# Masks and the first maximum behind self-attention's last turning, and the keys of batches 2 to 5 one step sooner

## The chip, the cores and the metric

The kernel runs on one core of a Trainium2 chip. The metric is the time of one execution in microseconds (us), taken on the device. Besides the plain timed runs there is one profiled execution, whose trace gives every instruction of every engine with its start and duration: TensorE (PE), VectorE (DVE), ScalarE (ACT), GpSimd (POOL), and SyncE (SP), which only issues DMAs.

## The reference

A stack of four attention blocks over x (8 batches, 256 positions, width 128) with a context of 8 x 64 x 64. The first two and the last are single cross-attention blocks. Nearly all of the work is the third, a decoder of six layers, each of which does:

```
tn = _ln(t, norm_g, norm_b)
t  = _mha(tn, tn, skv, sq, sow, sob, tgt_mask) + t      # self-attention, 16 heads of 64, 256 x 256 scores
tn = _ln(t, norm_g, norm_b)
t  = _mha(src, tn, ckv, cq, cow, cob, src_mask) + t     # cross-attention, 256 queries on 64 context rows
tn = _ln(t, pg, pb)
t  = t + (relu(tn @ w1 + b1) @ w2 + b2)                 # feed-forward, 512 wide
```

In `_mha` the scores are `q k^T / 8`, set to -1e9 where the mask is 0, then softmax, times the values, times the output weights. All is float32.

## The kernel before

**How work is put in order.** Every step of the kernel is a small Python function, put into a plan with `at(tick, phase, fn)`. At the end the plan is played by tick, and within a tick by phase, and the instructions of each engine are chained in just that order. So the order on each engine is written out by hand; what a step waits for beyond that follows from the data and from the buffers. Every PSUM tile, one or two banks, comes from one pool of four tiles (`psum`, line 30), which `two_banks`, `mm_tile` and `tp_tile` take in turn: a new tile waits until the one four places before it has been read out. SBUF tiles of 1024 columns come from a heap with four tiles for each tag ("q", "k", "v", "e", "o").

**A layer** has 48 ticks: self-attention takes four ticks for each of the eight batches, cross-attention two, from the tick that is called `T_ca`; its last stages, and the feed-forward, lap over into what follows.

**Self-attention** (`plan_sa`), for batch b at tick T. Two groups g of heads, four parts jj each. `scores` (PE, L946) fills a PSUM tile; `exps` adds the mask and takes the minimum (DVE, L960) and exponentiates (ACT, L965); `divide` takes the reciprocal (DVE, L973) and scales (POOL, L975, four instructions a part); `turn` transposes 32 x 32 blocks on DVE into `eTc` (L985, two instructions a part, each of which needs two of POOL's four scalings); `values(g)` (PE, L1001, 64 matmuls of two passes) multiplies with V into two PSUM tiles in turn, four matmuls to the first, four to the second, and so on; DVE copies the first out (L309) and ACT the second (L311). Then the output weights (L1019) and the sum with the residual (DVE, L1026). For the last batch, the last turn stands at tick `T_ca`, phase 2.2, and `values(1)` at tick `T_ca + 1`, phase 3.0.

**Cross-attention** (`plan_ca`, `plan_weights_64`), for batch b at T = T_ca + 2b:
- `keys_both` (for two batches, b even): folded keys on PE (L1138) into two PSUM tiles of two banks, copied by ACT (L1144, four instructions) into two "q" tiles.
- `mask_keys`: a tensor_tensor (L1152) that adds the context mask to the last 32 partitions of the batch's 1024 key columns, in place, on DVE.
- For each half qt of the queries at tick T + qt: `scores` (PE, L366, phase 1) into a PSUM tile; `lower` at phase 2, which copies it to SBUF (ACT, L377), takes the maximum of each head (DVE, L379) and subtracts it (POOL, L380); `exps` (ACT, L386, phase 8); one tick later `divide`, the sum and reciprocal (DVE, L390, L391) and the scaling (POOL, L392); two ticks later `turn` (DVE, L400); three ticks later `sums` (PE, L434) and the sum into t (DVE, L1170).
- `make_values` (PE, L328; ACT, L334), and `ahead`, the layer norm: statistics on DVE (L856 to L862), scale on POOL (L866, L869), normal form on ACT (L875), turned on PE (L889, tile `tp`) and copied by ACT (L891).

The mask of batch 0 stands at tick T_ca - 1, phase 1.9, and that of batch 1 at T_ca, phase 1.9. The keys of 2 and 3 stand at T_ca + 2, phase 3.7, their masks at T_ca + 3 and T_ca + 4, phase 1.9; the keys of 4 and 5 at T_ca + 6, phase 3.7.

Of the kernel before, what the change touches and what calls it, by code (L numbers as in the profile page):

```python
# [27 lines left out]
def tile_xattn_stack(ctx: ExitStack, tc: tile.TileContext, io, out: bass.AP):  # L28
    nc = tc.nc
# [15 lines left out]
    def two_banks(base):  # L45
        return psum.tile([P, 1024], F32, tag="ps", name=uniq(base))
# [10 lines left out]
    def big(tag, bufs=4, shape=(P, 1024), dtype=F32):  # L57

        return heap.tile(list(shape), dtype, tag=tag, name=uniq(tag), bufs=bufs)
# [244 lines left out]
    def at(tick, phase, fn):  # L304
        plan.setdefault(tick, []).append((phase, fn))
# [7 lines left out]
    def residual(b, bias):  # L313
        tb = sb([P, QT, D], "tb", 3)
        nc.gpsimd.tensor_tensor(
            tb, tt(b), bias.unsqueeze(1).to_broadcast([P, QT, D]), ALU.add
        )
        return tb

    def values_of(b, wvo):  # L320

        ps = two_banks("mm").rearrange("p (r k x) -> p r k x", r=2, k=2)
        w = wvo.rearrange("p (g a) d -> p a g d", g=2)
        for k in range(2):
            for a in range(4):
                for r in range(2):
                    rows = slice(r * DM, (r + 1) * DM)
                    nc.tensor.matmul(  # L328
                        ps[32 * a : 32 * a + 32, r, k, :],
                        lhsT=ctx2[rows, b, 32 * k : 32 * k + 32],  # L330
                        rhs=w[rows, a], start=True, stop=True,
                    )
        vw = big("v", shape=(P, 2, 2, 2, D))
        nc.scalar.copy(  # L334
            vw.rearrange("p r k g d -> p (r k g d)"), ps.rearrange("p r k x -> p (r k x)")
        )
        return vw

    def plan_weights_64(tick, qt, qT, keys, values, halves, take):

# [95 lines left out]
            take(ps)  # L438

        at(tick, 1, scores)  # L440
        at(tick, 2, lower)
        if halves:
            at(tick + 1, 2.05, exps)
            at(tick + 1, 2.5, turn)
# [245 lines left out]
    def plan_l0(b, T):  # L690
# [88 lines left out]
        for qt in range(QT):  # L779
            plan_weights_64(  # L780
                T + qt, qt, lambda: st["q"], lambda: st["k"], lambda: st["VW"], True,
                lambda ps, qt=qt: add(qt, ps),
            )
# [342 lines left out]
    def plan_ca(l, b, T):  # L1126
        st = {}
        fold = W["fold", l]

        def keys_both():  # L1130

            res = [big("q", shape=(D, 4, 4, M)) for _ in range(2)]
            for g in range(2):
                ps = two_banks("mm").rearrange("p (r a x) -> p r a x", r=2, a=4)
                for a in range(4):
                    for r in range(2):
                        rows = slice(r * DM, (r + 1) * DM)
                        nc.tensor.matmul(  # L1138
                            ps[:, r, a, :], lhsT=fold["AT"][rows, 4 * g + a, :],
                            rhs=ctx2[rows, b : b + 2, :].rearrange("p b m -> p (b m)"),  # L1140
                            start=True, stop=True,
                        )
                for i in range(2):
                    nc.scalar.copy(  # L1144
                        res[i][:, :, 2 * g : 2 * g + 2, :].rearrange("p a r k -> p r a k"),
                        ps[:, :, :, i * M : (i + 1) * M],
                    )
            keys_of[b], keys_of[b + 1] = res

        def mask_keys():  # L1150
            last = keys_of[b][96:].rearrange("p a c k -> p (a c) k")
            nc.vector.tensor_tensor(  # L1152
                last, last, nm2[96:, b].unsqueeze(1).to_broadcast([32, 16, M]), ALU.add
            )

        def make_values():
            st["VW"] = values_of(b, fold["WVO"])

        def res():
            st["tb"] = residual(b, W["ca", l][3])  # L1160

        ahead(b, (T - 5, 6), (T - 3, 2.95), (T - 2, 2.9), last_off, last_on, st)
        if b % 2 == 0:
            at(T - 2, 3.7, keys_both)
        at(T - 1 - b % 2, 1.9, mask_keys)
        at(T + 2, 3.2, make_values)
        at(T + 2, 7, res)

        def add(qt, ps):
            nc.vector.tensor_add(t[:, QT * b + qt, :], ps[:, :D], st["tb"][:, qt, :])  # L1170

        for qt in range(QT):
            plan_weights_64(
                T + qt, qt, lambda: st["tT"], lambda: keys_of[b], lambda: st["VW"],
                False, lambda ps, qt=qt: add(qt, ps),
            )

    def plan_ff(l, b, T, T_second, steps=None):
# [117 lines left out]
    for l in range(NL):  # L1296
        T_ca = T0 + 4 * B
        T_next = T_ca + 2 * B
        for b in range(B):
            plan_sa(l, b, T0 + 4 * b)  # L1300
        plan_ca_weights(l, T_ca - 7)
        for b in range(B):
            plan_ca(l, b, T_ca + 2 * b)
            T_ff = T_ca + 2 * b + 7
            if l + 1 < NL:
                plan_ff(l, b, T_ff, T_ff + 2)
            elif b < B - 2:
                plan_ff(l, b, T_ff, T_ff + 1)
            else:

                T_ff -= b - B + 3
                done = T_ca + 2 * b + 4
                plan_ff(
                    l, b, T_ff, T_ff + 1,
                    (4.6, (done, 6), (done, 8.7), (T_ff, 2.9)),
                )
            T_end[b] = T_ff + 1
        if l > 0:
            at(T0 + 8, -1, lambda l=l: load_ff(l))
        if l + 1 < NL:  # L1320
            at(T_ca + 4, -1, lambda l=l: load_sa(l + 1))
            at(T_next + 1, -1, lambda l=l: load_ca(l + 1))
        T0 = T_next
# [82 lines left out]
```

## Time and profile before

| what | value |
|---|---|
| plain runs | 2408.59, 2408.69 and 2411.47 us, median 2408.69 |
| the profiled execution | 2410.73 us |
| its span, first to last instruction | 2409.0 us |
| busy: PE, DVE, ACT, POOL | 2300.7, 1922.7, 1720.0, 1398.4 us |
| mean granted TensorE clock | 0.985 |
| one layer | 368.56 us |

The profiled execution is what every duration is taken from. "Busy" is the time in which an engine ran at least one instruction; PE's matmuls are pipelined, so a busy PE need not be at its peak, and a float32 matmul is recorded as two passes. The granted clock is the share of full speed that the chip let TensorE have; at 0.5 its matmuls take twice as long. In the timeline a row has its start, its length, the engine, the source line, the operation, the tiles (out<-in), the shapes and the count, and in brackets how long the engine stood idle before it and whose result ended that. In a view of windows a row has, for one stretch, its length, the busy time of PE, PE's weight loads, DVE, ACT and POOL with their instructions, the granted clock, and the DMA's share and rate.

### The profile page before, as it was taken

How to read it: one execution, taken by the hardware profiler on the slowest of the kernel's cores; microseconds unless marked ns; L12 is line 12 of the kernel's file. 1: busy time of each engine (PE TensorE's matmuls, PEld its weight loads, DVE VectorE, ACT ScalarE, POOL GpSimd, SP SyncE). 2: the span in 40 equal slices, each digit the busy share in tenths (PEclk: the TensorE clock that was granted, in tenths of full speed). 3: DMA queues.
4: the chain of work that ended last, by engine and by line, in shares of the span. 5: the costliest groups of instructions: out<-in, count | busy, mean ns of one | idle time of the engine just before them, and what ended most of it. 6: DMA issues, size and time to landing. Idle time of an engine off the chain costs nothing.

```text
span 2409.0 us, 97481 instructions
## 1 busy us (share of the span) xinstructions
PE 2300.7 (96%) x41124; PEld 1696.1 (70%) x41124; DVE 1922.7 (80%) x6269; ACT 1720.0 (71%) x4544; POOL 1398.4 (58%) x2243
## 2 busy tenths in 40 slices
PE   7889999999998999998999999899999899999897
PEld 3557776777776777776677777677777677777675
DVE  5678888967888967888877888877888877888885
ACT  4567777767777677777677778677778668777663
POOL 2445556854555864555865555865555774555774
PEclk9989999999999999999999999999999999999998
DMA  6000012001012001012001012000012000010000
GB/s 180 2 12 15 21 56 65 2 3 30 21 50 60 12 3 30 21 43 68 12 3 30 21 38 71 14 2 18 25 38 73 21 2 18 25 38 12 2 4 16
DMA packets 98932, 70.67 MB, mean 29 GB/s; under 512 B 7936, under 2 KB 93632, under 8 KB 98496
## 3 DMA queue, kind: packets, MB, share of 16 engines
q1 hardware_dynamic: 97904, 64.12, 9.9%
q8 instruction: 323, 5.29, 1.0%
q14 instruction: 113, 0.93, 0.1%
q10 hardware_dynamic: 592, 0.33, 0.1%
HBM read 59.19 MB, written 5.24 MB: 27 GB/s over the span
## 4 chain that ended last, share of the span: by engine, by line
PE 80%; DVE 11%; ACT 6%; issue 1%; POOL 1%; DMA 1%; SPq 0%; ACTq 0%; POOLq 0%; DVEq 0%
PE mm L909 14%; PE sc L946 13%; PE mm L1001 13%; PE mm L1019 7%; PE mm L928 7%; PE mm L434 6%; PE sc L366 4%; PE mm L1203 4%; PE mm L1186 3%; DVE m L379 2%; PE mm L328 2%; DVE e L960 2%; PE tp L889 2%; ACT e L965 1%; PE mm L1138 1%
## 5 line engine op out<-in xcount | busy, mean ns | idle before, releaser
L975 POOL TENSOR_SCALAR e<-e,rs 128x256 f32<-128x256 f32 x1536 | 714.8, 485 | 724.7 <-DVE rs L973 714.8
L965 ACT ACTIVATE e<-e,mn 128x256 f32<-128x256 f32 x1536 | 758.5, 495 | 145.5 <-DVE mn L960 144.6
L960 DVE CUSTOM_DVE_ANT_0 e<-sc,nm 128x256 f32<-128x256 f32 x1536 | 543.4, 419 | 116.7 <-PE sc L946 115.3
L985 DVE STREAM_TRANSPOSE eTc<-e 128x512 f32<-128x512 f32 x768 | 513.8, 693 | 54.0 <-POOL e L975 53.1
L1001 PE MATMUL mm<-eTc,v 32*64 32x256 f32 x12288 | 372.7, 385 | 25.1 <-DVE eTc L985 25.1
L946 PE MATMUL sc<-k,q 64*32 64x256 f32 x12288 | 380.5, 382 | 1.4 <-ACT v L311 0.6
L1001 PEld LDWEIGHTS mm<-eTc,v 32*64 32x64 f32 x12288 | 283.8, 134 | 111.0 <-issue 44.3
L380 POOL TENSOR_TENSOR e<-e,m 128x1024 f32<-128x1024 f32 x112 | 213.1, 1902 | 207.1 <-DVE m L379 206.8
L946 PEld LDWEIGHTS sc<-k,q 64*32 64x32 f32 x12288 | 221.7, 107 | 122.9 <-issue 45.9
L965 ACT ACTIVATION_READ_ACCUMULATOR e<-e,mn 128x1 f32 x1536 | 287.7, 187 | 0.0
L379 DVE TENSOR_REDUCE m<-e 128x16 f32<-128x1024 f32 x112 | 136.4, 1218 | 102.4 <-ACT e L377 100.3
L434 PE MATMUL mm<-v,o 128*128 128x128 f32 x1536 | 192.8, 279 | 18.7 <-DVE o L400 11.5
L434 PEld LDWEIGHTS mm<-v,o 128*128 128x128 f32 x1536 | 178.9, 192 | 41.4 <-issue 26.9
L909 PE MATMUL mm<-tT,w_sk 128*128 128x256 f32 x768 | 189.3, 389 | 0.0
L1019 PEld LDWEIGHTS mm<-w_sow,o 128*128 128x128 f32 x1536 | 175.1, 192 | 19.0 <-issue 12.3
L311 ACT COPY v<-mm 128x1024 f32<-128x1024 f32 x96 | 97.2, 1012 | 124.8 <-PE mm L928 124.8
L1019 PE MATMUL mm<-w_sow,o 128*128 128x128 f32 x1536 | 183.6, 278 | 2.8 <-ACT WVO L1100 2.8
L366 PE MATMUL sc<-q,tT 128*32 128x256 f32 x3072 | 185.5, 382 | 0.3 <-DVE t L1170 0.3
L928 PE MATMUL mm<-w_sv,tT 128*32 128x256 f32 x3072 | 185.6, 382 | 0.0
L392 POOL TENSOR_TENSOR e<-e,r 128x1024 f32<-128x1024 f32 x96 | 182.6, 1902 | 0.5 <-DVE r L391 0.5
L909 PE MATMUL mm<-tT,w_sq 128*128 128x256 f32 x768 | 173.6, 379 | 0.0
L909 PEld LDWEIGHTS mm<-tT,w_sk 128*128 128x128 f32 x768 | 138.2, 190 | 44.2 <-issue 29.2
(226 smaller groups left out, 3457.6 us busy)
## 6 DMA issues: line engine op xcount, KB each, us to landing
nm<-mask_d SPq DMA_DIRECT2D x192, 128.0 KB
w_sk<-in_L_sa_kv_dram SPq DMA_DIRECT2D x6, 512.0 KB
w_sv<-in_L_sa_kv_dram SPq DMA_DIRECT2D x24, 128.0 KB
w_sq<-in_L_sa_q_dram SPq DMA_DIRECT2D x6, 512.0 KB
w_sow<-in_L_sa_ow_dram SPq DMA_DIRECT2D x6, 512.0 KB
w_ckv<-in_L_ca_kv_dram SPq DMA_DIRECT2D x12, 256.0 KB
w_cq<-in_L_ca_q_dram SPq DMA_DIRECT2D x6, 512.0 KB
w_cow<-in_L_ca_ow_dram SPq DMA_DIRECT2D x6, 512.0 KB
```

Source lines behind the costliest of these rows:

```text
L366: nc.tensor.matmul(sc[32 * a : 32 * a + 32, q, :], lhsT=qT()[:, qb * 32 : (qb + 1) * 32], rhs=keys()[:, a].rearrange("p h k -> p (h k)"), ...
L380: nc.gpsimd.tensor_tensor(e, e, m.unsqueeze(2).to_broadcast([P, 16, M]), ALU.subtract)
L434: nc.tensor.matmul(ps[:, :D], lhsT=eT[:, s].rearrange("p q x -> p (q x)"), rhs=vw[:, r, k, g, :], start=(s == 0), stop=(s == 7),)
L909: nc.tensor.matmul(ps[:, i * S : (i + 1) * S], lhsT=w[:, c * P : (c + 1) * P], rhs=st["tT"], start=True, stop=True,)
L928: nc.tensor.matmul(ps[32 * a : 32 * a + 32, i, :], lhsT=st["tT"][:, kb * 32 : (kb + 1) * 32], rhs=sv[:, a].rearrange("p g x -> p (g x)"), ...
L946: nc.tensor.matmul(sc[32 * a : 32 * a + 32, r, j, :], lhsT=st["q"][g][rows, a, qb * 32 : (qb + 1) * 32], rhs=st["k"][g][rows, a, :], start ...
L960: nc.vector.tensor_tensor_reduce(e[:, i, :], sc4[:, i, :], st["nm"][:, 2 * jj + i % 2, :], -1.0, 3.0 * BIG, ALU.add, ALU.min, mn[:, i : i ...
L965: nc.scalar.activation(e[:, i, :], e[:, i, :], AF.Exp, scale=-1.0, bias=mn[:, i : i + 1], accum_out=rs[:, i : i + 1],)
L975: nc.gpsimd.tensor_scalar(e[:, i, :], e[:, i, :], rs[:, i : i + 1], 1.0, ALU.mult, ALU.mult)
L985: nc.vector.transpose(eT[:, r, :, 2 * jj : 2 * jj + 2, :], e[:, 2 * r : 2 * r + 2, :].rearrange("p j (k x) -> p k j x", x=32),)
L1001: nc.tensor.matmul(ops[a // 2][r * HD : (r + 1) * HD, a % 2, :S], lhsT=st["v"][kb // 4][rows, kb % 4, (2 * g + r) * HD : (2 * g + r + 1) * ...
L1019: nc.tensor.matmul(st["ps"][:, j * D : (j + 1) * D], lhsT=st["oT"][c // 4][:, c % 4, j * P : (j + 1) * P], rhs=sow[:, c, :], start=(c == 0 ...
```

## The change

```diff
-    def plan_weights_64(tick, qt, qT, keys, values, halves, take):
+    def plan_weights_64(tick, qt, qT, keys, values, halves, take, lower_at=2):
...
         at(tick, 1, scores)
-        at(tick, 2, lower)
+        at(tick, lower_at, lower)
...
         def mask_keys():
             last = keys_of[b][96:].rearrange("p a c k -> p (a c) k")
-            nc.vector.tensor_tensor(
+            (nc.vector if b else nc.gpsimd).tensor_tensor(
                 last, last, nm2[96:, b].unsqueeze(1).to_broadcast([32, 16, M]), ALU.add
             )
...
         if b % 2 == 0:
-            at(T - 2, 3.7, keys_both)
-        at(T - 1 - b % 2, 1.9, mask_keys)
+            at(*{2: (T - 3, 2.95), 4: (T - 3, 3.7)}.get(b, (T - 2, 3.7)), keys_both)
+
+        at(
+            *{0: (T - 1, 2.2), 1: (T - 2, 5.5), 2: (T - 2, 1.9), 3: (T - 4, 5.5)}.get(
+                b, (T - 1 - b % 2, 1.9)
+            ),
+            mask_keys,
+        )
...
             plan_weights_64(
                 T + qt, qt, lambda: st["tT"], lambda: keys_of[b], lambda: st["VW"],
                 False, lambda ps, qt=qt: add(qt, ps),
+                2.25 if b == 0 and qt == 0 else 2,
             )
```

In each of the six layers:
- The mask of batch 0 goes from DVE to POOL, at the same tick (T_ca - 1), phase 2.2.
- The mask of batch 1 stays on DVE and in tick T_ca, but at phase 5.5 instead of 1.9.
- `lower` of batch 0's first half goes from phase 2 to 2.25 of tick T_ca, so its copy, maximum and subtraction are issued after the last turn (phase 2.2) of self-attention.
- The keys of batches 2 and 3 go from T_ca + 2, phase 3.7, to T_ca + 1, phase 2.95, just ahead of self-attention's last `values(1)`; their masks go to T_ca + 2, phases 1.9 and 5.5.
- The keys of batches 4 and 5 go from T_ca + 6 to T_ca + 5, phase 3.7; their masks and those of 6 and 7 stay.

No instruction is added or removed but for the engine of the one mask. On DVE the new order around the last turn is: turn (L985, both), maximum (L379), mask of batch 1 (L1152), next maximum. On PE it is: scores, `tp`, scores, keys (L1138, two tiles), `values(1)`. On ACT the four key copies now come after the second L377 and before the copy (L311) that follows `values(1)`.

## The prediction

> **What bounds the kernel now.** I read the page first, then who waits for whom on the TensorE, then the timeline of the worst wait, then clock windows around it.
>
> ```profile
> PE 2300.7 (96%) x41124; PEld 1696.1 (70%) x41124; DVE 1922.7 (80%) x6269; ACT 1720.0 (71%) x4544; POOL 1398.4 (58%) x2243
> ...
> PE 80%; DVE 11%; ACT 6%; issue 1%; POOL 1%; DMA 1%; SPq 0%; ACTq 0%; POOLq 0%; DVEq 0%
> ```
>
> PE is the bound: only gaps in its queue, or its clock, can be won. Its waits (total us, times, longest):
>
> ```profile
> PE mm L1001 <- DVE eTc L985: 25.1, 12, 3.1
> ...
> PE mm L434 <- DVE o L400: 11.5, 12, 1.6
> PE mm L434 <- DVE t L1170: 6.3, 6, 1.1
> ```
>
> Times below are of layer 0; the layers repeat every 368.56 us (the 3.11 us wait ends at 404.98, 773.54 and so on to 2247.78). Where self-attention passes into cross-attention the timeline has
>
> ```profile
> 399.94 1.93 PE L366 MATMUL sc<-q,tT 128*32 128x256 f32 x32
> ...
> 400.33 1.27 DVE L985 STREAM_TRANSPOSE eTc<-e 128x512 f32<-128x512 f32 x2
> 400.51 2.80 POOL L975 TENSOR_SCALAR e<-e,rs 128x256 f32<-128x256 f32 x4 [0.19 <-DVE rs L973]
> ...
> 401.63 1.33 DVE L1152 TENSOR_TENSOR q<-q,nm 32x1024 f32<-32x1024 f32 x1
> 403.00 1.22 DVE L379 TENSOR_REDUCE m<-e 128x16 f32<-128x1024 f32 x1
> ...
> 404.13 1.29 DVE L985 STREAM_TRANSPOSE eTc<-e 128x512 f32<-128x512 f32 x2
> 404.29 1.90 POOL L380 TENSOR_TENSOR e<-e,m 128x1024 f32<-128x1024 f32 x1
> ...
> 404.98 5.89 PE L1001 MATMUL mm<-eTc,v 32*64 32x256 f32 x128 [3.11 <-DVE eTc L985]
> ...
> 406.23 1.06 ACT L386 ACTIVATE e<-e 128x1024 f32<-128x1024 f32 x1 [4.80 <-POOL e L380]
> 407.19 0.99 ACT L377 COPY e<-sc 128x1024 f32<-128x1024 f32 x1
> ```
>
> A mask (L1152) and the first maximum (L379) stand ahead of the last turning (404.13), and PE stands from 401.87 to 404.98. The values then take 5.89 us; the same 64 matmuls took 3.71 at 394.06. The windows (PE busy first, granted clock after POOL) say why:
>
> ```profile
> 402.60:406.00 3.40, 1.02 (x23) 0.64 (x31) 2.79 (x4) 0.00 (x0) 3.28 (x4) 1.00 0.00 0
> 406.00:409.40 3.40, 3.40 (x77) 2.56 (x69) 1.18 (x2) 2.73 (x4) 0.20 (x1) 0.50 0.02 5
> 409.40:412.80 3.40, 3.40 (x87) 1.98 (x72) 3.21 (x9) 1.54 (x2) 3.28 (x2) 1.00 0.00 0
> ```
>
> After a window that is 30% busy the clock is halved for the next 3.41 us: 1.7 us lost. The other 0.4 is the second half of the turning.
>
> **First mask to POOL.** DVE loses 1.22 us at 393.00. Its next work, L960, needs the first half of L946 (392.18 to 394.13), so it starts at 393.2 instead of 394.25. POOL's scaling before it ends at 393.60 instead of 394.56, since one of its instructions took 1.44 instead of 0.48 beside that mask. The mask takes 1.90 on POOL by L380 (the same 1024 columns, two SBUF operands), from 0.73 (L315) to 3.80 (twice L380). It waits for ACT's third key copy, which ends at 392.96, before POOL is free, and behind it stand only scalings. POOL has nothing to do until 397.4 and PE wants the keys at 397.70, so all of these are hidden; past 4.1 us each one costs one.
>
> **The last turning.** DVE's copy L309 now waits for PE's values (397.75, was 398.29). The statistics behind it take 1.96 as now, so the second reciprocal comes at 399.71 and POOL scales from 399.97, 4 x 0.455, to 401.8 (now 403.31, held by the mask at 401.63). The turning ends at 402.53, now 405.42.
>
> **Keys of 2 and 3.** L1138, 2.06 us of PE, moves from 417.64 to 401.87: PE is busy to 403.86, past the turning. So the 3.11 and the 0.4 go. ACT's four key copies (2.05) go with it; they now run 409.4 to 411.4, before the values end. No moved step issues a DMA, and none is moved past one that SP or POOL issues.
>
> **What is late next.** PSUM has four tiles, taken in turn (line 30). Now the sequence is values, values, scores, tp, scores, values, values: the last two take slots 2 and 3, long free. With two key tiles ahead of them they take slots 4 and 1, and slot 1 holds the second scores. These are emptied by ACT's second L377, which stands behind L386, which waits for L380, which waits for L379, now behind the turning. I follow it: L379 402.45 to 403.67. L380 would run 403.75 to 405.65, but the mask of batch 1 is now issued right behind L379, 0.05 us ahead of L380 (which starts 0.08 after L379's end). What that does, DVE first and POOL second, the timeline shows elsewhere (L290 alone takes 0.22):
>
> ```profile
> 2327.26 1.22 DVE L1152 TENSOR_TENSOR q<-q,nm 32x1024 f32<-32x1024 f32 x1
> 2327.28 1.29 POOL L290 TENSOR_SCALAR ve<-mv 128x2 f32<-128x2 f32 x1
> ```
>
> POOL is held until the mask ends. So L380 ends at 403.70+1.22+1.76=406.68 (1.76: the held L866 at 445.52 ended 0.55 after its mask, 0.15 less than its 0.70). L386 follows to 407.79, L377 to 408.68, the matmul at 408.75. Four of the 64 matmuls run at 403.8; PE then stands 4.7 us, and the other 60 take 3.48: 412.2, or 411.2 if POOL is not held.
>
> Then the clock. The grid of 3.41 us lies anywhere against a 4.7 us stand, because the layers no longer last 108 windows as they do now. In the layers, windows of 30 to 42% busy halved the next one, and those of 54% (429.9) did not. With a limit of one half, 1.05 to 2.6 us are lost, by where the grid falls: one whole busy window at half speed is 1.7, and a stand that covers most of two windows halves two. I take the middle, 1.9: values end at 414.1, now 410.87: **+3.25 us**.
>
> The Trainium skill (page TensorE: Matmul & The Clock Gate, Part 1, "What's actually happening") has the clock halved after at least one idle window. The row differs: 30% busy was enough. By the page a 4.7 us stand holds a whole idle window only where the grid's border falls in its first 1.3 us, 4 times in 10; the estimated loss would be 0.5 us instead of 1.9, and the sum -16 us. My sum goes by the row.
>
> **The ticks after,** counted from the end of the values. Without L1138 at +6.8 PE has its next scores at 8.70, not 10.68. From there, by the rows' durations: copy L377 to 9.80, L379 to 11.06, L390 and L391 to 12.47, first half of the turning of the batch's second half 13.04, L434 at 13.2, PE free at 12.84: wait 0.36 (as now). Next: scores 12.54, L386 and L377 to 15.03, L379 16.29, sum and reciprocal 17.7, turning 18.3, L434 18.42, PE free at 18.04: wait 0.38, now 1.56, as no mask (now 427.97, 1.25 us) stands ahead of that L379. The 1.05 wait is for a PSUM tile that L1170 empties; the new order has keys 4 and 5 there, copied at 24.6, PE free at 25.1: none. The scores now at +32.60 come at +28.05: **-4.5 us** (2.06 of L1138, 2.2 of waits, the rest overlap). Bounds: 2.06 with no wait gone, 5.0 with all. The masks of 2 and 3 lie on DVE at +1.9 and +7.0; the second is held by POOL's L392 to +8.3 and ends at +9.4, still ahead of L379 at 9.84. So each costs nothing there; if DVE were 0.5 us later, the waits of 0.36 and 0.38 would grow by as much.
>
> From there feed-forward joins, PE has no gap over 0.2 us, and the lead stays. Sum: 3.25-4.5=-1.25 a layer, times six **-7.5 us**. The profiled run is 2410.73 (span 2409.0 and 1.7 around it), giving 2403.2; the median of the runs lies 2.04 below it, so 2401.2.
>
> **Rivals.**
> POOL is not held, or slot 1 comes earlier: L377 at 407.65, values end 411.2+1.6=412.8, -2.6 a layer: 2393. Against it: the row at 2327.28.
> The change does all it says and no slot binds: values end 403.8+3.7=407.5, -7.9 a layer: 2361. Against it: the order of tiles, which is fixed.
> The waits cancel: the long stand costs two full half-clock windows, 3.4 us: +0.25 a layer, 2410.
> Slower: the half clock holds on. At the start of the program it lasted 6.83 us three times, once through a window (88.56) in which PE was 68% busy. If three windows follow each stand, 4.1 us are lost, +0.95 a layer: 2414.4. It costs from 3.2 us of loss on, and over 0.2% from 4.0. Against it: in layers 0 to 5 it never lasted over 3.41.
>
> **Numbers.** Forecast 0.50 (with 1.05 to 2.6 us of clock, -2.1 to -0.55 a layer, -12.6 to -3.3 us, about a quarter of it within 0.2%); POOL free 0.22; all gained 0.04; cancel 0.12; slower 0.12. 0.2% (4.8 us) is about what a measurement can tell here. Faster 0.38+0.22+0.04=0.64; same 0.12+0.12=0.24; slower 0.12. Range 2390 (POOL free with 1.05 us of clock, -3.1 a layer) to 2412 (the cancelling case, 2410, with some of the slower one); it leaves out the case in which all is gained and most of the slower one, 0.14.
>
> **What would show it.** Right: no wait of L1001 for L985 over 0.2 us in the boundary; instead one of some 4.7 us for ACT's L377, inside the values; the last turning near 402.5; L380 there 2.9 us long; L434's 1.56 under 0.5; half-clock windows still in every layer. Wrong: L380 at 1.90 (then 2393), the wait for L377 absent, two or three half windows a layer, or a POOL mask past 4 us.

## The result and the profile after

The changed kernel takes 2413.98 us (median of 19 runs, 2412.7 to 2415.34), the kernel before 2409.87 us beside it (19 runs, 2406.2 to 2412.77). The ratio is 1.0015, its 95% interval 1.0008 to 1.0021: slower by 0.15%, some 3.6 us (the medians are 4.1 us apart), where 7.5 us less had been forecast. The profiled execution has a span of 2412.3 us (2409.0 before) and a mean granted clock of 0.984.

From the page of the changed kernel, the busy times and the chain that ended last, by engine:

```profile
PE 2298.5 (95%) x41124; PEld 1695.5 (70%) x41124; DVE 1916.6 (79%) x6263; ACT 1720.0 (71%) x4544; POOL 1413.2 (59%) x2249
...
PE 78%; DVE 10%; ACT 5%; POOL 3%; issue 2%; DMA 1%; SPq 0%; ACTq 0%; POOLq 0%; DVEq 0%
```

The six masks have left DVE for POOL. PE's share of the chain fell by two hundredths and POOL's rose by two: PE waits more, not less. Who it waits for (total us, times, longest):

```profile
PE mm L1001 <- ACT e L377: 24.3, 6, 4.1
PE mm L434 <- DVE o L400: 10.2, 22, 1.1
PE mm L1001 <- DVE eTc L985: 6.8, 6, 1.1
...
PE tp L889 <- DVE t L1176: 6.3, 7, 1.0
```

The waits for the last turning are gone (25.1 in 12 before, 6.8 in 6 now; what is left belongs to the other values), and so is L434's wait of 6.3 for L1170. In their place stand 24.3 for L377 and 6.3 for L1176. By these rows alone PE waits 4.7 us more than before: 24.3 + 10.2 + 6.8 + 6.3 = 47.6 against 25.1 + 11.5 + 6.3 = 42.9. (Lines below 1161 have moved down by 6 or 7; L1176 is the old L1170.)

**At the boundary** of layer 0 all is as forecast. The whole execution is 2.47 us late when it comes here, from the start-up, whose code is the same: 1.61 us at 27.5 us, where DVE has waited 4.58 us for the DMA of a parameter (`L_norm_g`) and only 2.54 in the kernel before, and most of the rest at 34 to 45 us, where a half clock lasts 6.83 us instead of 3.41. The timeline:

```profile
404.74 1.18 DVE L379 TENSOR_REDUCE m<-e 128x16 f32<-128x1024 f32 x1
...
405.95 1.22 DVE L1152 TENSOR_TENSOR q<-q,nm 32x1024 f32<-32x1024 f32 x1
406.00 2.93 POOL L380 TENSOR_TENSOR e<-e,m 128x1024 f32<-128x1024 f32 x1 [0.99 <-DVE m L379]
...
408.96 1.06 ACT L386 ACTIVATE e<-e 128x1024 f32<-128x1024 f32 x1 [5.26 <-POOL e L380]
409.93 0.99 ACT L377 COPY e<-sc 128x1024 f32<-128x1024 f32 x1
...
410.97 5.37 PE L1001 MATMUL mm<-eTc,v 32*64 32x256 f32 x120 [4.06 <-ACT e L377]
```

The mask is issued 0.05 us ahead of L380 and holds it: 2.93 us instead of 1.90. L386 and the second copy L377 follow, and PE stands 4.06 us for the PSUM tile that this copy empties. Two windows around it (PE busy first, granted clock after POOL):

```profile
408.50:411.90 3.40, 0.93 (x34) 0.81 (x42) 0.95 (x1) 2.94 (x5) 0.43 (x1) 1.00 0.00 0
411.90:415.30 3.40, 3.40 (x75) 2.60 (x67) 1.65 (x3) 1.73 (x4) 3.05 (x2) 0.50 0.02 5
```

A window 27% busy is followed by one at half clock. From the start of the first values to the end of the second pass 19.81 us; before it was 16.81.

**Seven ticks on** the profile leaves the forecast. The timeline of the changed kernel:

```profile
448.00 1.65 DVE L1152 TENSOR_TENSOR q<-q,nm 32x1024 f32<-32x1024 f32 x1
...
449.68 1.22 DVE L379 TENSOR_REDUCE m<-e 128x16 f32<-128x1024 f32 x1
...
450.98 1.90 POOL L380 TENSOR_TENSOR e<-e,m 128x1024 f32<-128x1024 f32 x1 [0.50 <-DVE m L379]
...
452.92 1.06 ACT L386 ACTIVATE e<-e 128x1024 f32<-128x1024 f32 x1 [0.63 <-POOL e L380]
453.40 0.25 DVE L1176 TENSOR_TENSOR t<-mm,tb 128x128 f32<-128x128 f32 x1
...
453.70 0.44 PE L889 MATMUL tp<-ident,xn 128*128 128x128 f32 x2 [1.04 <-DVE t L1176]
...
453.88 0.99 ACT L377 COPY e<-sc 128x1024 f32<-128x1024 f32 x1
```

This is one half of the queries. The mask of batch 4 stands on DVE ahead of the maximum L379; POOL, then ACT's exponential, then the next copy wait for that in turn, and PE waits for DVE's addition behind it. 1.08 us follow at 459.90, for L400. The windows say what DVE has to spare there (the third busy time). The changed kernel:

```profile
447.00:453.90 6.90, 5.64 (x55) 3.78 (x54) 6.68 (x14) 5.09 (x12) 6.32 (x6) 1.00 0.00 0
453.90:460.70 6.80, 5.72 (x89) 4.10 (x89) 6.63 (x13) 3.83 (x6) 6.22 (x6) 1.00 0.01 2
```

and the kernel before in the like half (last row) and the three ahead of it:

```profile
427.00:433.40 6.40, 4.84 (x82) 3.22 (x81) 6.23 (x13) 3.37 (x5) 4.94 (x5) 1.00 0.00 0
433.40:438.80 5.40, 4.27 (x49) 2.73 (x49) 5.16 (x15) 3.68 (x8) 5.32 (x6) 1.00 0.01 3
438.80:445.60 6.80, 6.80 (x114) 5.10 (x113) 6.49 (x18) 5.80 (x11) 6.23 (x7) 1.00 0.01 2
445.60:452.30 6.70, 6.47 (x64) 4.80 (x64) 6.50 (x14) 4.91 (x11) 6.12 (x5) 1.00 0.00 0
```

In the like half DVE is busy 97% in both. Before, PE was too (6.47 of 6.70), so no wait showed. Now PE is ready sooner, and what it won at the tick before it spends waiting. The first two rows of before show which of the two sets the pace: there DVE is as full (6.23 of 6.40, 5.16 of 5.40) while PE is not (4.84 and 4.27). Row by row, from 422.8 us (the maximum behind the fourth copy) to 465.4, DVE has no gap over 0.08 us in the kernel before; it is busy 40.56 of 42.60 us, and the rest lies in small gaps between its instructions. So DVE had nothing to spare there.

### The profile page after: what moved, and what is told of

Its sections match the earlier page's. It is cut to its first block, busy times and chain, and to the rows that moved or that the text cites. A ratio compares the mean times of both kernels' runs of the same rounds, so it can differ in the third digit from the quotient of the medians.

```text
span 2412.3 us, 97516 instructions
## 1 busy us (share of the span) xinstructions
PE 2298.5 (95%) x41124; PEld 1695.5 (70%) x41124; DVE 1916.6 (79%) x6263; ACT 1720.0 (71%) x4544; POOL 1413.2 (59%) x2249
## 4 chain that ended last, share of the span: by engine, by line
PE 78%; DVE 10%; ACT 5%; POOL 3%; issue 2%; DMA 1%; SPq 0%; ACTq 0%; POOLq 0%; DVEq 0%
PE mm L1001 14%; PE sc L946 14%; PE mm L909 14%; PE mm L1019 7%; PE mm L928 7%; PE mm L434 5%; PE mm L1210 3%; PE sc L366 3%; PE mm L1193 3%; DVE m L379 2%; ACT e L965 1%; PE tp L889 1%; PE mm L328 1%; DVE o L400 1%; DVE r L390 1%
## 5 line engine op out<-in xcount | busy, mean ns | idle before, releaser
L975 POOL TENSOR_SCALAR e<-e,rs 128x256 f32<-128x256 f32 x1536 | 703.2, 478 | 711.4 <-DVE rs L973 701.5
L985 DVE STREAM_TRANSPOSE eTc<-e 128x512 f32<-128x512 f32 x768 | 513.8, 693 | 55.1 <-POOL e L975 54.1
L1001 PE MATMUL mm<-eTc,v 32*64 32x256 f32 x12288 | 374.1, 386 | 31.1 <-ACT e L377 24.3
L1001 PEld LDWEIGHTS mm<-eTc,v 32*64 32x64 f32 x12288 | 281.7, 135 | 118.4 <-issue 28.5
L380 POOL TENSOR_TENSOR e<-e,m 128x1024 f32<-128x1024 f32 x112 | 219.2, 1957 | 203.8 <-DVE m L379 203.8
L379 DVE TENSOR_REDUCE m<-e 128x16 f32<-128x1024 f32 x112 | 136.2, 1216 | 106.3 <-ACT e L377 104.6
L434 PE MATMUL mm<-v,o 128*128 128x128 f32 x1536 | 192.2, 279 | 10.4 <-DVE o L400 10.2
L434 PEld LDWEIGHTS mm<-v,o 128*128 128x128 f32 x1536 | 178.9, 192 | 31.9 <-issue 27.7
L311 ACT COPY v<-mm 128x1024 f32<-128x1024 f32 x96 | 97.2, 1013 | 124.8 <-PE mm L928 124.8
L366 PE MATMUL sc<-q,tT 128*32 128x256 f32 x3072 | 185.5, 382 | 0.3 <-DVE t L1176 0.3
L392 POOL TENSOR_TENSOR e<-e,r 128x1024 f32<-128x1024 f32 x96 | 182.6, 1902 | 0.5 <-DVE r L391 0.5
```

What stands on the lines that cost most here:

```text
L366: nc.tensor.matmul(sc[32 * a : 32 * a + 32, q, :], lhsT=qT()[:, qb * 32 : (qb + 1) * 32], rhs=keys()[:, a].rearrange("p h k -> p (h k)"), ...
L380: nc.gpsimd.tensor_tensor(e, e, m.unsqueeze(2).to_broadcast([P, 16, M]), ALU.subtract)
L434: nc.tensor.matmul(ps[:, :D], lhsT=eT[:, s].rearrange("p q x -> p (q x)"), rhs=vw[:, r, k, g, :], start=(s == 0), stop=(s == 7),)
L975: nc.gpsimd.tensor_scalar(e[:, i, :], e[:, i, :], rs[:, i : i + 1], 1.0, ALU.mult, ALU.mult)
L985: nc.vector.transpose(eT[:, r, :, 2 * jj : 2 * jj + 2, :], e[:, 2 * r : 2 * r + 2, :].rearrange("p j (k x) -> p k j x", x=32),)
L1001: nc.tensor.matmul(ops[a // 2][r * HD : (r + 1) * HD, a % 2, :S], lhsT=st["v"][kb // 4][rows, kb % 4, (2 * g + r) * HD : (2 * g + r + 1) * ...
```

## The experiments

**The theories.** Theory 1: from some tick of cross-attention on, the copies L377 follow each other at a pace of their own. Copy, maximum, subtraction and exponential take 0.99 + 1.22 + 1.90 + 1.06 = 5.17 us and the next copy stands behind the exponential on ACT; DVE's own work for a half (L379, L390, L391, L400 twice, L1176, the statistics) takes about as long (it is busy 5.00 of the 5.20 us from 430.4 on). PE needs less, so PE's lead is waited away. Rival B: the stand for the PSUM tile is what costs. Rival C: it is the copies of keys 4 and 5 (L1144), now ahead of an exponential on ACT.

The table holds what the answers below refer to: starts of L377 in layer 1's cross-attention, counted from the first, in us; the time from the fourth to the eleventh; the mean length of the first five layers, from first copy to first copy; the median. From the eleventh copy to the sixteenth it is 41.3 to 41.5 us in every kernel. The first copy of layer 0 came anywhere from 399.5 to 403.3 us, though the start-up's code is the same, so medians of few runs differ by a few us by that alone, and the length of a layer is the finer measure.

| kernel | 2nd | 3rd | 4th | 4th to 11th | a layer | median |
|---|---|---|---|---|---|---|
| before | 7.23 | 12.84 | 21.75 | 42.65 | 368.56 | 2409.9 to 2411.1 |
| changed | 7.70 | 16.05 | 22.92 | 42.21 | 368.97 | 2414.0 |
| e1 keys 4, 5 back | 7.71 | 16.59 | 23.46 | 41.37 | 368.76 | 2413.5 |
| e2 values first | 7.72 | 14.72 | 22.46 | 42.23 | 368.66 | 2412.7 |
| e3 second copy first | 2.18 | 11.82 | 18.46 | 42.43 | 364.87 | 2390.1 |
| e4 no masks 4, 5 | 7.71 | 15.89 | 22.77 | 39.84 | 367.21 | 2403.2 |
| e5 = e3 + mask 1 later | 2.18 | 10.79 | 17.43 | 42.47 | 363.87 | 2383.7 |
| e6 = e3 + e1 | 2.18 | 11.83 | 18.46 | 41.62 | 364.08 | 2382.1 |
| e7 before + second copy first | 1.95 | 12.86 | 21.77 | 42.66 | 368.64 | 2411.0 |
| e8 all copies first | 2.18 | 11.59 | 18.42 | 41.38 | 364.15 | 2382.0 |
| e9 boundary alone | 7.72 | 12.94 | 22.48 | 42.65 | 369.30 | 2414.8 |
| e10 keys alone | 7.24 | 15.59 | 22.46 | 42.22 | 369.12 | 2413.6 |
| e11 = e5 + e1 | 2.18 | 10.77 | 17.41 | 41.61 | 362.98 | 2379.8 |
| e12 = e8 + mask 1 later | 2.18 | 10.53 | 17.36 | 41.39 | 363.09 | 2378.0 |

**e1, keys of 4 and 5 back.**

```diff
-            at(*{2: (T - 3, 2.95), 4: (T - 3, 3.7)}.get(b, (T - 2, 3.7)), keys_both)
+            at(*{2: (T - 3, 2.95)}.get(b, (T - 2, 3.7)), keys_both)
```

> The changed kernel (2414.0 us), with the keys of batches 4 and 5 back at their old place, one tick later. Theory 1 (from tick T_ca+5 to T_ca+9 the chain of ACT's copy L377, DVE's maximum L379, POOL's L380 and ACT's L386, on a DVE that has no idle time from 444 to 466 us, sets the pace, so PE's lead of some 2 us is waited away): the 0.92 us that DVE stands at 442.82 behind the key copies goes, the two masks stay, so 0.5 to 0.9 us a layer come back: 2408.5 to 2411 us. Rival B (the stand of 4.06 us for the PSUM slot is all that costs): nothing changes, 2414. Rival C (the copies of keys 4 and 5, 2.0 us ahead of L386 on ACT, give the lead away): all of it comes back, some 2.4 us a layer, 2400.

2413.5 us; ratio to before 1.0007 (0.9998 to 1.0017). The stretch behind the fourth copy is 0.84 us shorter, as theory 1 had it, and L434 waits 1.05 us for L1176 again, as before. In the whole little of it shows, since this execution had half-clock stretches of 6.83 us instead of 3.41 in four of its six boundaries, and so a later fourth copy. The time is above what theory 1 expected and near rival B's 2414, and it is the stretch that speaks for theory 1; rival C, which wanted 2.4 us a layer, falls, but its mechanism is real and worth a third of that.

**e2, values ahead of the keys.**

```diff
-            at(*{2: (T - 3, 2.95), 4: (T - 3, 3.7)}.get(b, (T - 2, 3.7)), keys_both)
+            at(*{2: (T - 3, 3.05), 4: (T - 3, 3.7)}.get(b, (T - 2, 3.7)), keys_both)
```

> The changed kernel, with the keys of batches 2 and 3 right behind the second values instead of ahead of them, so that the values get the two PSUM tiles that are long free. In the trace PE waits some 0.6 us for the last turning, then runs the values in one piece; the second key tile waits about 1.1 us for L377; PE is 4 us or more further at the next scores of layer 0 than in the changed kernel. Rival B (the slot costs it): 4.3 us a layer come off, 2388 us. Theory 1 (the later ticks are paced by the softmax chain and DVE): PE's lead grows to some 6 us after the values and is waited away by tick T_ca+9, the layer ends as in the changed kernel: 2412 to 2416. Rival C: as theory 1, about 2414.

2412.7 us; ratio 1.0003 (0.9994 to 1.0011). The values run in one piece, at 404.87. Yet the next scores start at 414.81, counted from the first copy 2.1 us sooner than in the changed kernel (11.98 after it, against 14.04) and not 4: PE waits 1.31 us for L377 among the keys and 2.05 for DVE's copy L309, which stands on DVE behind the second maximum, and that behind the second copy. A window 40% busy there is again followed by one at half clock. Rival B doesn't hold: without its 4.06 us stand, and with PE 2.1 us ahead at these scores, a layer is 0.3 us shorter and not 4.3.

**e3, the second copy ahead of the first exponential** (`lower_at` differs from 2 in batch 0's first half alone).

```diff
-            at(tick, 8, exps)
+            at(*((tick, 8) if lower_at == 2 else (tick + 1, 2.05)), exps)
```

> The changed kernel, with one step moved: ACT's exponential L386 of the first half of batch 0 stands behind the copy L377 of the second half, so that this copy doesn't wait for POOL and the PSUM tile is free some 5 us sooner. In the trace the 4.06 us wait of L1001 for L377 is gone or under 0.5, and so is the half-clock window behind it. Rival B: 4.06 and some 1.7 of clock, 5.8 us a layer, 2379 us. Theory 1: the whole lead is waited away in ticks T_ca+5 to T_ca+9, 2411 to 2416, with longer waits of L434 for L400 and L889 for L1176 in layer 0 than the 1.08 and 1.04 of the changed kernel.

2390.1 us; ratio 0.9915 (0.9902 to 0.9929). Neither number was right, and here theory 1 had to be mended. The timeline of e3:

```profile
404.24 1.01 ACT L377 COPY e<-sc 128x1024 f32<-128x1024 f32 x1 [0.70 <-PE sc L366]
...
406.09 3.71 PE L1001 MATMUL mm<-eTc,v 32*64 32x256 f32 x128
...
411.65 1.93 PE L366 MATMUL sc<-q,tT 128*32 128x256 f32 x32 [1.85 <-ACT q L1144]
```

The second copy no longer waits for POOL, the values need 3.71 us, and no half-clock window is left at the six boundaries. But the waits of 0.25, 1.03 and 1.08 further on are the same as in the changed kernel, to 0.01, and the stretch from the fourth copy on has its 42.4 us. What came sooner is the fourth copy itself, by 4.5 us, and with it the whole train. So theory 1 stands in this form: **from the fourth copy on the layer runs at a pace of its own; a change pays by as much as it brings that copy forward**, and PE's lead is of use only where it does so. In PE's rows the 24 us are 11.9 of waits (35.7 now, 47.6 in the changed kernel: the same rows, with 11.1 of L366 for L1144 in place of L1001's 24.3 for L377) and some 11.9 of half clock (23.9 us of it in the boundaries of the changed kernel, none here; half of it is lost where PE is busy throughout).

**e4, without the masks of batches 4 and 5** (left out, so two batches' cross-attention is unmasked).

```diff
...
+        if b not in (4, 5):
+            at(
...
```

> The changed kernel without the masks of batches 4 and 5 (their cross-attention is left unmasked). Theory 1: DVE is relieved of 2 x 1.65 us a layer just in the ticks where it has no idle time and where each mask stands ahead of L379; the waits of 1.04 (L889 for L1176) and 1.08 (L434 for L400) go, the lead stays, 2.0 to 2.4 us a layer: 2399.5 to 2402 us. Rival B (the stand for the slot) and rival C (the key copies ahead of L386): both stay as they are, no more than 0.3 us a layer, 2412 to 2414.

2403.2 us; ratio 0.9963 (0.9951 to 0.9976). The 1.04 and 1.08 are gone, the stretch is 2.37 us shorter, as theory 1 had it; the whole is 1.2 us over its range, as three of the six boundaries had 6.83 us of half clock (such a layer lasted 367.5 to 367.9 us, the others 366.4 and 366.6).

**e5, the mask of batch 1 behind the second maximum,** on top of e3.

```diff
-            *{0: (T - 1, 2.2), 1: (T - 2, 5.5), 2: (T - 2, 1.9), 3: (T - 4, 5.5)}.get(
+            *{0: (T - 1, 2.2), 1: (T - 1, 2.2), 2: (T - 2, 1.9), 3: (T - 4, 5.5)}.get(
```

> The changed kernel with the copy L377 of batch 0's second half ahead of its first exponential (2390.1 us), and the mask of batch 1 moved from right behind the first maximum L379 to right behind the second. POOL's first L380, 2.94 us long in that kernel, takes 1.90, and the first L386 comes 1.0 us sooner; with it ACT's key copies, the scores that wait 1.85 us for them, and all copies L377 behind. Theory 1, as the run before has mended it (from the fourth copy L377 of cross-attention on, the softmax chain and DVE run at a fixed pace of 5.2 us a half, whatever PE's lead, so only what makes that copy come sooner shortens the layer): 1.0 us a layer, 2384 us. Rival (only PE's standing for the slot counted, and it is gone): no change, 2389 to 2391. Rival: the mask holds the second L380 instead and the first L386 gains nothing: 2389 to 2392.

2383.7 us; ratio 0.9884 (0.9868 to 0.9899), 6.4 us less than e3. The timeline of e5 (two L380 in one row, 4.75 us together):

```profile
406.09 4.75 POOL L380 TENSOR_TENSOR e<-e,m 128x1024 f32<-128x1024 f32 x2 [0.98 <-DVE m L379]
...
407.17 1.91 DVE L1152 TENSOR_TENSOR q<-q,nm 32x1024 f32<-32x1024 f32 x1
408.02 1.06 ACT L386 ACTIVATE e<-e 128x1024 f32<-128x1024 f32 x1 [2.53 <-POOL e L380]
```

The first L380 ends at 408.0, 1.9 after its start; now the mask is held, to 1.91, and it holds the second L380 in turn (2.88 us). That costs nothing: the second L380 ends 8.5 us behind the first copy, in e3 8.6. The third and the fourth copy come 1.03 us sooner: the mended theory to a tenth.

**e6, e3 with the keys of 4 and 5 back** (the diffs of e1 and e3).

> The same kernel of 2390.1 us with the keys of batches 4 and 5 back at their old place. Theory 1: the sixth to the last copy L377 of a layer come some 0.8 us sooner, as in the changed kernel with these keys back (82.86 us from the fourth to the last copy there against 83.68), and with no half-clock windows at the boundary this shows in the whole: 5 us, 2385. Rival (the place of these keys costs nothing): 2390.

2382.1 us; ratio 0.9878 (0.986 to 0.9896). A layer is 0.79 us shorter than e3's, as expected; the profiled spans differ by 4.2 (2386.5 and 2382.3), the medians of four runs each by 7.9.

**e7, the kernel before with that one step of e3** (`first` is true for batch 0's first half alone).

```diff
-            at(tick, 8, exps)
+            at(*((tick + 1, 2.05) if first else (tick, 8)), exps)
```

> The kernel before, with that one step moved (the second copy L377 of batch 0 ahead of the first L386) and nothing else. Theory 1: there the third copy waits for PE's scores, which stand behind the last turning and the values, so a sooner second copy changes nothing: 2409 to 2412 us, and the step pays only together with the change. Rival (the step alone is worth the 24 us): 2387.

2411.0 us; ratio 1.0001 (0.9992 to 1.001). The second copy comes 5.3 us sooner and the third not at all: before, the third waits for PE's scores, behind the last turning. So the change did take a limit away; the second copy was the next one, right behind it.

**e8, every exponential behind the next copy.**

```diff
-            at(tick, 8, exps)
+            at(tick + 1, 2.05, exps)
```

> The changed kernel with every exponential L386 of cross-attention behind the copy L377 of the next half, not batch 0's alone (2390.1 us). Then the chain copy, maximum, subtraction, exponential is no longer closed by ACT's queue. If that chain of 5.17 us (0.99 + 1.22 + 1.90 + 1.06) sets the pace: halves follow each other in less than 5.2 us, the key copies and the masks lose their weight, up to 2.4 us a layer, 2376 us. If DVE's own work sets it (L379, L390, L391, L400 twice, L1176 and the statistics, 5.22 us a half without idle): the spacing stays 5.2 and 6.9 us, only the 0.92 us behind the key copies goes, 2385 us. Rival: L386 now waits for the next scores, so L390, L400 and L434 come later and PE waits more: 2393 or above.

2382.0 us; ratio 0.9875 (0.9862 to 0.9889). The time lies between the two expected ones, nearer to that of DVE. The edit opens the loop on ACT; in layer 0 the copies now wait for PE's scores in 10 of 12 places instead of 3. The stretch shortens by 1.05 us, near the 0.92 of the key copies and far from 2.4. The windows of e8, half by half (DVE is the third busy time):

```profile
425.80:430.90 5.10, 4.96 (x82) 3.33 (x82) 4.96 (x15) 2.82 (x3) 4.71 (x6) 1.00 0.01 3
...
443.20:450.00 6.80, 6.19 (x81) 4.12 (x87) 6.61 (x13) 5.10 (x10) 6.22 (x6) 1.00 0.00 0
```

From 425.8 to 460.5 DVE is busy 33.74 of 34.70 us, and what is left are gaps of 0.02 to 0.04 between instructions. Its maxima follow each other by 5.05, 5.40, 6.87, 6.87 and 5.06 us, near the 5.2 and 6.9 expected of DVE. With the loop open, DVE's own work sets the pace, and it is about the same pace.

**e9, the boundary's part alone** (keys and masks of batches 2 to 5 as before; the diff is against the changed kernel).

```diff
-            at(*{2: (T - 3, 2.95), 4: (T - 3, 3.7)}.get(b, (T - 2, 3.7)), keys_both)
+            at(T - 2, 3.7, keys_both)
...
-            *{0: (T - 1, 2.2), 1: (T - 2, 5.5), 2: (T - 2, 1.9), 3: (T - 4, 5.5)}.get(
+            *{0: (T - 1, 2.2), 1: (T - 2, 5.5)}.get(
```

> The kernel before with the boundary's part of the change alone: first mask on POOL, the first lowering behind the last turning, the second mask behind it; keys and masks of batches 2 to 5 stay. PE then waits some 0.6 us for the last turning instead of 3.11, and the values lie in tiles that are free, so PE is 4.5 us ahead after the values. As the working on record would count it (what PE wins there stays): 2383 us. Theory 1 (the copies L377 set the layer): the second copy is late by half a microsecond (7.7 behind the first, 7.23 before), the third stands behind the second L386, some 13.0 behind the first as before (12.85); PE's lead is waited away at that copy: 2408 to 2412 us.

2414.8 us; ratio 1.0018 (1.0009 to 1.0027). The third copy stands at 12.94, as expected from the softmax chain, though PE is done with the values at 407.14. It then waits at two places, here the second:

```profile
412.07 0.63 DVE L309 COPY o<-mm 128x512 f32<-128x512 f32 x1
...
412.75 1.06 ACT L386 ACTIVATE e<-e 128x1024 f32<-128x1024 f32 x1 [2.02 <-POOL e L380]
412.75 1.65 PE L1019 MATMUL mm<-w_sow,o 128*128 128x128 f32 x6 [2.11 <-DVE o L309]
```

0.93 us and 2.11 us, and a half-clock window after them: 3.04 in place of the 3.11 that went. The fourth copy is 0.73 us later than before, which put the time above the expected range.

**e10, the keys' part alone** (masks 0 and 1 and the first lowering as before; keys of 2 to 5 and masks of 2 and 3 as in the change; the diff is against the changed kernel).

```diff
-            (nc.vector if b else nc.gpsimd).tensor_tensor(
+            nc.vector.tensor_tensor(
...
-            *{0: (T - 1, 2.2), 1: (T - 2, 5.5), 2: (T - 2, 1.9), 3: (T - 4, 5.5)}.get(
+            *{2: (T - 2, 1.9), 3: (T - 4, 5.5)}.get(
...
-                2.25 if b == 0 and qt == 0 else 2,
+                2,
```

> The kernel before with the other part alone: keys of batches 2 to 5 one tick sooner, masks of 2 and 3 behind them; boundary as before. The values then need the tile of the second scores, which is free at 408.2 in layer 0: PE stands some 2.5 us there and the values end 2.5 us later than before. If a stand of PE counted as such: 2425 us. Theory 1: the fourth copy L377 comes 0 to 0.6 us later than before (21.75 behind the first), then 1.2 us are won where no mask stands ahead of the sixth and 0.8 lost to the copies of keys 4 and 5: 2408 to 2413 us.

2413.6 us; ratio 1.0009 (1.0 to 1.0017), 0.6 us above what theory 1 expected. The values wait 1.14 us for the turning and 2.10 for L377's tile; the fourth copy is 0.71 us late, the stretch 0.43 shorter.

**e11, e3's step, e5's mask and e1's keys together.**

> The changed kernel with the three edits that paid: second copy L377 of batch 0 ahead of the first L386, mask of batch 1 behind the second maximum (6.4 us in a run), keys of 4 and 5 at their old place (7.9 us in a run). Theory 1: the first two move the start of the fixed-pace stretch, the third shortens the stretch itself, so they add: 2390.1 - 6.4 - 7.9 = 2376 us. Rival (both won the same wait): 2381 to 2384.

2379.8 us; ratio 0.9875 (0.986 to 0.989), between the two expected times. A layer lasts 362.98 us: 1.00 less by the mask and 0.89 less by the keys, which add to within 0.1 us of the single steps (1.00 and 0.79). The median came down by 10.3 and not by the 14.3 that the medians of e5 and e6 promise, in part because those held chance of the start-up (the first copy is at 403.25 here, 401.12 in e6).

**e12, e8 with e5's mask.**

> The changed kernel with every L386 of cross-attention behind the next copy L377 (2382.0 us), and the mask of batch 1 behind the second maximum. Theory 1, with DVE as what sets the pace there (it had no idle time from 425.8 to 460.5 us of that run): the whole stretch starts 1.0 us sooner, 2376 us. Rival (the copy is no longer held by L386, so the first L380 doesn't count): 2382.

2378.0 us; ratio 0.9867 (0.9854 to 0.9881), the fastest of all: 33 us below the kernel before beside it (2411.0), and 2.0 above what theory 1 expected. The fourth copy comes 1.06 us sooner than in e8 and the stretch stays (41.39): the first L380 counts here too.

## Why the prediction was wrong, by its own steps

**First mask to POOL: in effect right.** It takes 2.37 us there, not 1.90, and is hidden as forecast; the limit was 4.1.

**The last turning: right.** It ends at 404.82, which is 402.35 on the clock of before; 402.53 was forecast. PE never waits for it.

**What is late next, and the clock: right.** The PSUM tile binds in every layer, 4.06 us for the 4.7 forecast, L380 is held to 2.93, and a half-clock window follows, 3.41 us in five layers and 6.83 in one. The values end 3.0 us later than before; 3.25 was forecast.

**The ticks after: right up to the point where they were counted.** The scores forecast at +28.05 behind the values' end come at +27.65; L434's waits are 0.28 and 0.32 (0.36 and 0.38 forecast) and the 1.56 and 1.05 are gone. At that point a layer of the changed kernel is 1.96 us ahead, more than the 1.25 that the sum used.

**The step that failed is the last one: "From there feed-forward joins, PE has no gap over 0.2 us, and the lead stays."** In the next three halves PE gives back 0.25 + 0.17 + 1.04 + 1.08 = 2.54 us, and a layer ends 0.2 to 0.5 us later than before. That PE had no gap there in the kernel before was read as if nothing else were near its limit. But DVE had no gap over 0.08 us there either, from the fourth copy's maximum on, and the prediction's premise "PE is the bound: only gaps in its queue, or its clock, can be won", taken from shares of the whole run (PE 96%, DVE 80%), did not hold in this stretch. The windows of before show it (DVE 6.50 of 6.70 beside PE's 6.47, 5.16 of 5.40 beside PE's 4.27); the prediction went by windows of the boundary. e4 shows the cause from one side (less on DVE there, 2.37 us back) and e3 from the other (PE and the copies earlier together: the same waits, and the layer 4.1 us shorter than the changed kernel's).

**Keys of 4 and 5: priced on PE alone.** The prediction saw that their tiles delay no matmul. Their copies, 2.0 us on ACT, stand ahead of an L386 that POOL had released at 439.95; it runs at 440.80, and DVE stands 0.92 us for the copy behind. The seventh L377 is 6.15 us behind the sixth, 5.34 before: 0.81 us a layer, which e1 and e6 give back (0.84 and 0.81).

So a layer's account goes by copies, not by PE's gaps (layer 1): the fourth copy 1.17 later; no mask ahead of the sixth's maximum, -1.27 from fourth to sixth; key copies, +0.81; from there to the eleventh, +0.02; 0.73 in all. 0.2 of it is won back in self-attention; 0.53 stay in layers 0 to 2, 0.2 to 0.3 in 3 and 4. In the profiled pair these five layers make 2.04 us, what follows gives 1.0 back, and 2.27 of the span's 3.3 lie ahead of the first copy, the DMA at the start above all, which is chance. So the edits account for about 1.0 of the 4.1 us between the medians; how the rest comes about is not settled. The half clock may have a part in it: e1 and e4 have the changed boundary and show 6.83 us of it in four and three layers, where the profiled execution has it once, and the fourth copy of such a layer comes later by 0.5 to 0.7 us in e1, about 1.2 in e4 and about 1.5 in the changed kernel.

**The rivals on record.** The slower case, a half clock that holds on for three windows, didn't occur: no boundary of the changed kernel has over 6.83 us of it. Nor did the waits cancel by two half-clock windows behind each stand: that came in one layer of six. The time came out on the slower side by another road, a new wait in place of the old one some seven ticks later, for which no rival had been written. That all is gained and no slot binds (-7.9 a layer) was tried by e3, with the slot freed: a layer is 3.7 us shorter than before (364.87 against 368.56), half of it.

The Trainium skill (page SBUF — State Buffer, section "SBUF: two separate sides") calls the port pair of DVE and GpSimd an exclusive lock that one instruction keeps to its end. The rows agree: L380, 0.05 us behind the mask, took 2.93 instead of 1.90; in e5, with L380 first, the mask took 1.91 instead of 1.22. The prediction had this from a row, and rightly so.

The page Perfetto Trace Analysis (section "Optimizing Scalar/DVE Operations") warns that moving work between DVE and GpSimd may not help where DVE is saturated, since they share that port. Here the mask of batch 0 on POOL did no harm, as POOL was idle; in the saturated halves, where POOL is busy 6.32 of 6.90 and 6.22 of 6.80 us, no run tried it.

## What to carry to other kernels

A lead of one engine is worth something only as far as the next engine behind it has slack, so ahead of "the lead stays" read the busy time of every engine in the windows that follow, and above all where the bound has no gaps: here 97% beside a full PE, with no gap over 0.08 us, meant that two engines were at the limit. Follow the train that repeats (here copy, maximum, subtraction, exponential, copy) and ask of each edit whether it moves the train's start or its pace. Where a local gain vanishes, look for what else stands in front of the same start: here one exponential ahead of one copy on ACT hid 24 us.

## What the runs showed of the hardware that was not expected

The mask of 32 partitions and 1024 columns took 2.37 us on POOL, where L380, with four times the partitions and as many columns, takes 1.90. On DVE the same mask takes 1.22 us alone and 1.65, 1.91 or 2.32 beside POOL's two-input instructions, by how much of one is left when it is issued (2.32 behind L392 at 423.14).

A window of 3.41 us with PE 27% busy halved the next one here, and so did one 40% busy whose longest stand was 2.05 us (e2); stands of 0.8 us in the same place (e11, e12) and of 1.85 us (e3, e8) halved none.
